# One written order over all blocks, scalings first in their chunk, and a re-dealt second block in a time-mix and FFN kernel

## The chip, the core and the metric

The kernel runs on one NeuronCore of one Trainium2 chip. The metric is the device time of one execution in microseconds (us); lower is better. PE is TensorE (its matmuls; PEld its weight loads), DVE is VectorE, ACT is ScalarE, POOL is GpSimd, and SP (SyncE) issues nearly all of the DMAs. Each engine has its own queue of instructions; between engines semaphores make an instruction wait.

## The reference

The input x has the shape 4 x 1024 x 512 (batch, time, channels); there are 704 hidden channels in the time mix and 2048 in the FFN. Cut to what matters:

```python
xn  = layernorm(x)
xx  = concat([xn[:, 1:2], xn[:, :-1]], axis=1) - xn        # the token before
k   = (xn + xx * time_mix_k) @ Wk.T
r   = (xn + xx * time_mix_r) @ Wr.T
w   = exp(-exp(time_decay))
s_t = s_{t-1} * w + relu(k_t)                              # a scan over time, per hidden channel
o   = layernorm((s * r) @ Wv.T) * ln_gamma + ln_beta
d   = gelu(fp16(xn) @ W0.T + bias0).astype(fp16)
e   = (d @ W1.T + bias1).astype(fp16)
out = x + o + e
```

## The kernel before

The 4096 tokens are worked on in eight blocks of 512 tokens, two to a batch (TB = 512), counted from 0; block i is mixed, projected, scanned and gated, and goes through the FFN. The loop over the blocks has 16 chunks n (NN = 16), one for each 128 of the FFN's hidden channels. In a chunk PE does `up` for the FFN chunk two ahead (AHEAD = 2, 8 matmuls into a bank pd, L784), `down` for chunk n (8 matmuls into the four sums pe, L806) and one piece of the time mix. After the last chunk DVE rounds the four sums pe to fp16 (`rounded`, L763, called e in the profile), which frees them for the next block's first `down`.

A piece is, in blocks from the second on, one of ten `three_pass` projections (bank pa, L626, and bank pb by `product`, L383): k in chunks 0 to 4, r in chunks 7 to 11, with two half passes in chunks 5 and 6. In chunks 12 to 15 the pieces are the four output products: `out_three_pass` (oa, L721; ob, L729 and L731) from the third block on, and `out_full` with `out_halves` in the first two. What follows a piece on ACT and DVE, its `after`, is issued in the chunk behind it: ACT copies pa (L638, or oa at L735), DVE adds pb (L639, or L736), and then come the relu (L641) and the scan (L519) for k, and the gating (L536) for r. The pool `ps_mm` has four PSUM banks for pd, pa, pb, oa and ob; the pool `ps_e` has four more for pe.

Exact fp32 products are made of parts. `split_x` makes three (h by ACT at L284, l and m by DVE at L286 and L288, with a first step at L235), `split_kr` does it for the weights of k and r and stores the parts to DRAM, `split_wv` for those of the output. Parts are tiles of 128 x 512 in buffers of tag "q" (QS of them; a block's states g, raw weights and the FFN's w0h and w0l take them too), and a new part waits until the buffer it gets has been read for the last time. Short-lived fp32 tiles (`temp`) have the tag "s".

The next block, j = i + 1, is made ready in the meantime: x is loaded, DVE takes its statistics, normalizes it, and transposes it in 16 steps into xnT (L331). `x16` has ACT copy xnT to fp16 (L344), `ffn_input` copies that to the FFN's input xf (L379). `mixed` is run for each of four groups of channels c: ACT scales the current token twice (L360), DVE adds the scaled token before (L363 and L367; in the first block of a batch a one-column copy, L352, comes first), and `split_x` follows.

The order on PE, DVE, ACT and SP is the written one, by `manual_schedule`; it holds within a region, and the loop opens one region for each block. Where instructions of two regions fall among each other, and POOL's order, are left to the scheduler. Within a chunk the written order is: `up`, the first step of the followers, Gelu and its cast (L794, L799), `down`, the piece, and then the rest of the followers woven with the chunk's list of background jobs `bg[n]`, which `put(n, ...)` fills.

Of the kernel before, what the change touches and what calls it, by code (L numbers as in the profile page):

```python
# [11 lines left out]
F32 = mybir.dt.float32  # L12
F32R = mybir.dt.float32r
I32 = mybir.dt.int32
AF = mybir.ActivationFunctionType
ALU = mybir.AluOpType

P = 128
# [4 lines left out]
def time_mix_and_gelu_ffn(  # L23
# [30 lines left out]
    nc = tc.nc  # L54
# [3 lines left out]
    TB = 512  # L58
    NS = TB // P
    NC = C // P  # L60
    NN = N // P
    Q = 32
    QS = 63
    RAW_OUT = 2
    S = 4096.0
    MASK = -4096
# [6 lines left out]
    LAST = len(blocks) - 1  # L73
# [5 lines left out]
    const = pool("const", 1)  # L79
# [5 lines left out]
        return wide.tile([P, TB], dtype, tag=tag, name=name, bufs=bufs)  # L85

    def temp(name):
        return const.tile([P, TB], F32, tag="s", name=name, bufs=5)

    def small(shape, tag, name, bufs=2):  # L90
        return const.tile(shape, F32, tag=tag, name=name, bufs=bufs)
# [246 lines left out]
    def half_tile(name):  # L338
        return const.tile([P, TB], F16, tag="h16", name=name, bufs=NS)

    def x16(i):
        for c in range(NC):
            x16s[i, c] = half_tile(f"x16_{i}_{c}")
            nc.scalar.copy(x16s[i, c], xnT[:, c, 1:])  # L344

    def mixed(i, c, meanwhile=lambda: None):
        t0 = blocks[i][1]
        now = xnT[:, c, 1:]
        if t0 > 0:
            nc.gpsimd.tensor_copy(xnT[:, c, 0:1], last[:, c, :])  # L350
        else:
            nc.vector.tensor_copy(xnT[:, c, 0:1], now[:, 0:2][:, 1:2])  # L352
        if t0 + TB < T:
            nc.gpsimd.tensor_copy(last[:, c, :], xnT[:, c, TB : TB + 1])
        prior = xnT[:, c, :TB]
        srcs = []
        for kind in range(2):
            j = kind * NC + c
            srcs.append(temp(f"x{'kr'[kind]}_{i}_{c}"))
            nc.scalar.activation(srcs[kind], now, AF.Identity, scale=rest_sb[:, j : j + 1])  # L360
        xk, xr = srcs
        meanwhile()
        nc.vector.scalar_tensor_tensor(  # L363
            xk, prior, mk_sb[:, c : c + 1], xk, ALU.mult, ALU.add
        )
        yield
        nc.vector.scalar_tensor_tensor(  # L367
            prior, prior, mr_sb[:, c : c + 1], xr, ALU.mult, ALU.add
        )
        xks[i, c] = yield from split_x(xk, f"k_{i}_{c}")  # L370
        xrs[i, c] = prior
# [4 lines left out]
    def ffn_input(i):  # L376
        xf = [part(f"xf_{i}_{c}", tag="xf", bufs=4) for c in range(NC)]
        for c in range(NC):
            nc.scalar.copy(xf[c], x16s.pop((i, c)))  # L379
        return xf  # L380
# [464 lines left out]
    def several(fn, *calls):  # L845
        for args in calls:
            fn(*args)
# [16 lines left out]

    followers = []
    e16s = []
    for i in range(len(blocks)):
        with tc.manual_schedule(
            engines=engines
        ):  # L870
            j = i + 1
            tail = 4 if i == LAST else 0
            by_columns = range(NS // 2, NS) if tail else ()
            pieces, bg = {}, defaultdict(list)

            def put(n, fn, *args):
                bg[n].append(lambda: fn(*args))
# [15 lines left out]

            def turn(first, end):
                transposed(state["x"], first, end)

            def fresh_mixed(c, n):
                if i > 0 and n == NN - AHEAD - 1:
                    return mixed(j, c, next_xf)
                return mixed(j, c)  # L900

            def next_xf():
                state["xf"] = ffn_input(j)

            for s in range(NS):
                pieces[12 + (s // 2 if i == LAST else s), s] = [out_piece, i, s]
            if i == 0:
                state["x"] = x_next
                pieces[1, 0] = [raw_k, i, 3]
                pieces[3, 0] = [raw_r, i, 3]  # L910
                pieces[5, 0] = [raw_k, i, 4]
                pieces[7, 0] = [raw_r, i, 4]
                pieces[9, 0] = [
                    lambda i: raw_halves(i, [bank(f"pkr_{i}_{q}") for q in range(2)]), i
                ]
                put(0, several, split_w0, (1, 2), (1, 3))
                for c in range(NC):
                    put(2 + c - (c == 0), split_w0, 2, c)
                    put(3 + c, load_w0, 3, c)
                    put(5 + c, split_w0, 3, c)  # L920
                put(1, stats, *range(NS))
                put(3, lambda: norm_apply(j, state["x"]))
                for h in range(NF):
                    put(1 + 2 * h, split_kr, 0, h)
                put(4, turn, 0, 1)
                put(5, turn, 1, 5)
                put(7, turn, 5, 10)
                put(8, turn, 10, 11)
                put(9, turn, 11, 16)
                put(4, load_late_constants)  # L930
                put(12, split_half)
                mix_at = (11, 12, 13, 15)
            else:
                order = [(0, h) for h in range(NF)] + [(1, h) for h in range(NF)]
                for k, (kind, h) in enumerate(order):
                    pieces[k + 2 * kind, 0] = [three_pass, i, kind, h]
                    if k > 1:
                        early = (4, 6, 8, 9, 10)[h] if i == kind == 1 else k - 2 + 2 * (k > 6)
                        put(early, fetch_kr, i, kind, h)
                pieces[5, 0] = [half_pass, i, 0]  # L940
                pieces[6, 0] = [half_pass, i, 1]
                for c, n in enumerate((2, 3, 5, 5) if i == 1 else (2, 2, 3, 3)):
                    put(n, split_xr, i, c)
                if j <= LAST:
                    put(2, fetch_x)
                    for s in range(NS):
                        put(4, stats, s)
                    put(6 if i == 1 else 5, lambda: norm_apply(j, state["x"]))
                    turns = (0, 5, 5, 5, 1) if i == 1 else (3, 4, 4, 3, 2)
                    for k in range(sum(turns)):  # L950
                        unit = next(n for n in range(5) if k < sum(turns[: n + 1]))
                        put(6 + unit, turn, k, k + 1)
                mix_at = (12, 13, 15, 15) if i == 1 else (12, 13, 14, 15)
            if i == 1:
                for g in range(NN // G):
                    put(2 * g, store_w0l, g)
                for h, n in enumerate((1, 10, 11, 12, 13, 13)):
                    put(n, split_wv, h)
            put(11 if j <= LAST else 2, fetch_residual)
            if j <= LAST:  # L960
                put(10, x16, j)
                for c, n in enumerate(mix_at):
                    put(n, fresh_mixed, c, n)
                put(13, fetch_kr, j, 0, 0)
                put(14, fetch_kr, j, 0, 1)

            pe = [ps_e.tile([P, C], F32, tag="pe", name=f"pe_{i}_{s}") for s in range(NS)]
            for n in range(NN):
                ahead = n + AHEAD
                if ahead == NN and j <= LAST:  # L970
                    if i == 0:
                        next_xf()
                    xf = state["xf"]
                nxt = (i, ahead) if ahead < NN else (j, ahead - NN)
                gelu = up(*nxt) if nxt[0] <= LAST else None
                works = [follow() for follow in followers]
                if i == 0 or n == NN - NS or (n > NN - NS and i < RAW_OUT):
                    finished(*works)
                    works = []
                else:  # L980
                    works = [w for w in works if next(w, works) is None]
                followers = []
                if gelu:
                    d = gelu()
                if n < NN - tail:
                    operands = waiting.pop(0)
                    for s in range(NS):
                        down(n, s, *operands, end=NN - tail if s in by_columns else NN)
                if gelu and i > 0:
                    waiting.append((d, load_w1(*nxt)))  # L990
                two_on = (i, ahead + 2) if ahead + 2 < NN else (j, ahead + 2 - NN)
                if two_on[0] <= LAST:
                    load_w0l(*two_on)
                jobs = [
                    lambda s=s: finish(i - 1, s, e16s[s])
                    for s in (2 * n, 2 * n + 1)
                    if s < len(e16s)
                ]
                for s in range(NS):
                    if (n, s) in pieces:  # L1000
                        fn, *args = pieces[n, s]
                        followers.append(fn(*args))
                if i == 0 and ahead + 1 < NN:
                    load_w1_raw(ahead + 1)
                woven(works, jobs + bg[n])
                if i == 0:
                    waiting.append((d, load_w1(*nxt)))
                store_weights()
# [60 lines left out]
```

## Time and profile before

| | us |
|---|---|
| median of 3 runs | 886.42 (885.8 to 887.17) |
| the profiled execution | 889.37 |
| its span, first to last instruction | 887.2 |
| the first `down` of blocks 2 to 7 (counted from 0) begins at | 252.29, 357.58, 462.93, 568.25, 673.62, 778.96 |

The last row is from the chain of waits: from block 2 on a block takes 105.3 to 105.4 us. Busy time by stage, where each row is a stretch of the span, followed by the busy time of each engine and the number of its instructions, the granted TensorE clock, the share of the DMA engines and what they moved:

```profile
44.00:137.00 93.00, 92.32 (x361) 59.69 (x360) 68.21 (x113) 50.84 (x87) 4.73 (x10) 1.00 0.68 232
137.00:249.20 112.20, 109.28 (x442) 80.76 (x440) 85.40 (x140) 58.28 (x97) 5.53 (x14) 0.98 0.67 220
453.30:558.60 105.30, 104.96 (x461) 86.01 (x461) 84.36 (x135) 51.41 (x86) 11.72 (x20) 1.00 0.66 225
```

They are most of the first block, the second block, and one of the later ones. The columns of busy time are PE, PEld, DVE, ACT and POOL. A matmul's shown duration (0.39 us) is longer than the distance between the starts of two (0.23 us), so waits of PE are best read from starts.

### The profile page before, as it was taken

To read this page: it belongs to the slowest core of one execution; us is meant where nothing else is said; L and a number is where in the kernel's file an instruction comes from. 1 tells how busy PE (TensorE), PEld (TensorE's weight loads), DVE (VectorE), ACT (ScalarE), POOL (GpSimd) and SP (SyncE) were. 2 spreads that over 40 slices of the span, in tenths; PEclk is the share of its full clock that TensorE was granted. 3 is DMA by queue.
4 is the path that set the end of the run, shared out by engine and by line. 5 is a ranking of instruction groups with operands and counts; after the bars stand their busy time and mean duration, and the time that the engine had idled before them with its cause. 6 is when DMAs were issued, how large, how long until landed. Compare 5 with 4: busy or idle time off the path is not lost.

```text
span 887.2 us, 11092 instructions
## 1 busy us (share of the span) xinstructions
PE 868.7 (98%) x3760; PEld 686.6 (77%) x3760; DVE 671.3 (76%) x1098; ACT 431.5 (49%) x733; POOL 75.2 (8%) x142
## 2 busy tenths in 40 slices
PE   8999999999999999999999999999999999999996
PEld 7676657876668888788878888788887888878885
DVE  4767768697698868878697787877788886884547
ACT  3856653456534455444554445444464445544430
POOL 1100000000012001000112000100011200100001
PEclk8999999999999999999999999999999999999998
DMA  9579755965449675677458775596665966568731
GB/s 261 202 226 326 250 170 177 327 231 192 152 139 353 208 225 175 228 267 243 163 170 300 234 238 190 169 337 197 216 201 182 328 208 223 179 221 279 236 120 48
DMA packets 100164, 195.01 MB, mean 220 GB/s; under 512 B 10991, under 2 KB 25356, under 8 KB 100108
## 3 DMA queue, kind: packets, MB, share of 16 engines
q1 hardware_dynamic: 100048, 194.29, 65.7%
q8 instruction: 30, 0.49, 0.2%
q14 instruction: 26, 0.21, 0.1%
q10 hardware_dynamic: 60, 0.02, 0.0%
HBM read 165.43 MB, written 28.84 MB: 219 GB/s over the span
## 4 chain that ended last, share of the span: by engine, by line
PE 80%; DVE 10%; ACT 4%; DMA 2%; issue 2%; SPq 0%; ACTq 0%; DVEq 0%
PE pd L784 22%; PE pe L806 21%; PE pa L626 13%; PE pb L383 7%; PE oa L721 5%; PE po L682 3%; PE ph L655 2%; PE ob L729 2%; PE pk L383 2%; DVE xnT L331 2%; PE pr L383 1%; PE ob L731 1%; ACT d L794 1%; DMA wvraw<-in_L_attn_Wv 1%; DVE e L763 1%
## 5 line engine op out<-in xcount | busy, mean ns | idle before, releaser
L806 PE MATMUL pe<-w,d 128*128 128x512 f32 x1008 | 252.5, 392 | 3.3 <-DVE e L763 1.7
L806 PEld LDWEIGHTS pe<-w,d 128*128 128x128 f32 x1008 | 187.2, 188 | 49.5 <-DVE e L763 9.2
L784 PE MATMUL pd<-xf,w0h 128*128 128x512 f32 x512 | 204.5, 399 | 0.3 <-ACT xf L379 0.3
L784 PE MATMUL pd<-xf,w0l 128*128 128x512 f32 x512 | 199.9, 390 | 0.0
L794 ACT ACTIVATE d<-pd,late_sb 128x512 f16<-128x512 f32 x128 | 87.7, 685 | 131.7 <-PE pd L784 131.4
L784 PEld LDWEIGHTS pd<-xf,w0h 128*128 128x128 f32 x512 | 96.5, 189 | 27.1 <-issue 4.1
L784 PEld LDWEIGHTS pd<-xf,w0l 128*128 128x128 f32 x512 | 96.6, 189 | 21.7 <-issue 1.9
L639 DVE SCALAR_TENSOR_TENSOR y<-pb,a 128x512 f32<-128x512 f32 x70 | 48.3, 690 | 66.7 <-PE pb L383 52.3
L638 ACT ACTIVATE a<-pa 128x512 f32<-128x512 f32 x70 | 41.7, 596 | 86.6 <-PE pa L626 86.6
L799 ACT CAST d<-d 128x512 fp32r<-128x512 f16 x128 | 79.5, 621 | 4.1
L331 DVE STREAM_TRANSPOSE xnT<-x 32x512 f32<-32x512 f32 x112 | 78.6, 702 | 2.0
L299 POOL TENSOR_SCALAR ry<-mvy 128x1 f32<-128x1 f32 x32 | 20.2, 630 | 436.2 <-DVE mvy L306 436.2
L626 PE MATMUL pa<-hk,kr 128*128 128x512 f32 x140 | 54.5, 390 | 0.0
L626 PE MATMUL pa<-lk,kr 128*128 128x512 f32 x140 | 54.5, 389 | 0.0
L363 DVE SCALAR_TENSOR_TENSOR xk<-xnT,mix_sb,xk 128x512 f32<-128x512 f32 x28 | 21.1, 752 | 34.1 <-ACT xk L360 34.0
L626 PE MATMUL pa<-hr,kr 128*128 128x512 f32 x120 | 46.7, 389 | 0.0
L721 PE MATMUL oa<-wv,lg 128*128 128x512 f32 x120 | 46.7, 389 | 0.0
L721 PE MATMUL oa<-wv,hg 128*128 128x512 f32 x120 | 46.7, 389 | 0.0
L626 PE MATMUL pa<-lr,kr 128*128 128x512 f32 x120 | 46.7, 389 | 0.0
L641 ACT ACTIVATE y<-y 128x512 f32<-128x512 f32 x35 | 22.1, 633 | 49.4 <-DVE y L639 49.4
L519 DVE TENSOR_TENSOR_SCAN g<-late_sb,carry,y 128x512 f32<-128x512 f32 x20 | 25.7, 1284 | 18.3 <-ACT y L641 13.3
L383 PE MATMUL pb<-mk,kr 128*128 128x512 f32 x140 | 37.4, 389 | 0.0
(166 smaller groups left out, 1348.7 us busy)
## 6 DMA issues: line engine op xcount, KB each, us to landing
w<-w1d SPq DMA_DIRECT2D x110, 512.0 KB, 3.7
kr<-krd SPq DMA_DIRECT2D x195, 256.0 KB, 4.9
w0l<-w0d SPq DMA_DIRECT2D x96, 256.0 KB, 4.0
x<-in_L_attn_x SPq DMA_DIRECT2D x32, 256.0 KB, 6.0
w1d<-w SPq DMA_DIRECT2D x16, 512.0 KB, 2.9
xres<-in_L_attn_x SPq DMA_DIRECT2D x32, 256.0 KB, 5.3
krd<-wt SPq DMA_DIRECT2D x30, 256.0 KB, 3.2
out<-xres SPq DMA_DIRECT2D x28, 256.0 KB, 4.6
```

Source lines behind the costliest of these rows:

```text
L331: nc.vector.transpose(dst[i * Q : (i + 1) * Q, :, :, j, :], src[j * Q : (j + 1) * Q, :, :, i, :],)
L383: return nc.tensor.matmul(dst, w[:, c, :], src, start=(c == 0), stop=(c == NC - 1))
L519: nc.vector.tensor_tensor_scan(dst[:hw], w_sb[:hw, h : h + 1].to_broadcast([hw, TB]), src[:hw], 0.0 if t0 == 0 else carry[:hw, h : h + 1], ...
L626: nc.tensor.matmul(pa, w[p][:, c, :], xs[j, c][p], start=(c == 0 and p == 0), stop=(c == NC - 1 and p == 1),)
L638: nc.scalar.activation(a, pa, AF.Copy, scale=1.0 + 1.0 / S)
L639: nc.vector.scalar_tensor_tensor(y, pb, -1.0 / S, a, ALU.mult, ALU.add)
L682: nc.tensor.matmul(pos[s], gs[i, h][:, s * P : (s + 1) * P], wv_raw[h], start=(h == 0), stop=False,)
L721: nc.tensor.matmul(pa, gs[i, h][p][:, cols], wv[h][p], start=(h == 0 and p == 0), stop=(h == NF - 1 and p == 1),)
L784: nc.tensor.matmul(pd, w, xf[c], start=(c == 0 and p == 0), stop=(c == NC - 1 and p == 1),)
L794: nc.scalar.activation(d16, pd, AF.Gelu, bias=b0_sb[:, n : n + 1])
L799: nc.scalar.copy(d, d16)
L806: nc.tensor.matmul(pe[s] if sum_ is None else sum_, d[:, s * P : (s + 1) * P], w1[p][:, cols], start=(n == first and p == 0), stop=(n == e ...
```

## The change

All blocks now stand in one `manual_schedule` region, so that the written order holds from block to block. `mixed` loses its two scalings; they become `scaled_now`, which is issued at the head of the chunk, ahead of the followers and Gelu, except where two groups are mixed in one chunk: there the second is scaled just before it is mixed. The fp16 copies are put two to a chunk (chunks 10 and 11 in the first block, 11 and 12 later; all four in chunk 10 before). `ffn_input` is run in chunk 13 behind Gelu (in chunk 14 ahead of `up` in the first block before, and inside `mixed` in chunk 13 in the others). In the second block (i == 1) the splits of r's input go to chunks 1, 2, 3, 4 (2, 3, 5, 5 before), its statistics to chunks 4 and 5 two each (all to 4 before), the first split of Wr to 5 (4 before) and the first of Wv to 7 (1 before). One buffer moves from tag "q" (63 to 62) to tag "s" (5 to 6).

```diff
-    QS = 63
+    QS = 62
...
     def temp(name):
-        return const.tile([P, TB], F32, tag="s", name=name, bufs=5)
+        return const.tile([P, TB], F32, tag="s", name=name, bufs=6)
...
-    def x16(i):
-        for c in range(NC):
-            x16s[i, c] = half_tile(f"x16_{i}_{c}")
-            nc.scalar.copy(x16s[i, c], xnT[:, c, 1:])
-
-    def mixed(i, c, meanwhile=lambda: None):
+    def x16(i, c):
+        x16s[i, c] = half_tile(f"x16_{i}_{c}")
+        nc.scalar.copy(x16s[i, c], xnT[:, c, 1:])
+
+    parts_now = {}
+
+    def scaled_now(i, c):
+        parts_now[i, c] = [temp(f"x{k}_{i}_{c}") for k in "kr"]
+        for kind, dst in enumerate(parts_now[i, c]):
+            j = kind * NC + c
+            nc.scalar.activation(
+                dst, xnT[:, c, 1:], AF.Identity, scale=rest_sb[:, j : j + 1]
+            )
+
+    def mixed(i, c):
...
-        srcs = []
-        for kind in range(2):
-            j = kind * NC + c
-            srcs.append(temp(f"x{'kr'[kind]}_{i}_{c}"))
-            nc.scalar.activation(srcs[kind], now, AF.Identity, scale=rest_sb[:, j : j + 1])
-        xk, xr = srcs
-        meanwhile()
+        xk, xr = parts_now.pop((i, c))
...
-    for i in range(len(blocks)):
-        with tc.manual_schedule(
-            engines=engines
-        ):
+    with tc.manual_schedule(engines=engines):
+        for i in range(len(blocks)):
...
-            pieces, bg = {}, defaultdict(list)
+            pieces, bg, early = {}, defaultdict(list), defaultdict(list)
...
-            def fresh_mixed(c, n):
-                if i > 0 and n == NN - AHEAD - 1:
-                    return mixed(j, c, next_xf)
-                return mixed(j, c)
-
-            def next_xf():
-                state["xf"] = ffn_input(j)
...
-                        early = (4, 6, 8, 9, 10)[h] if i == kind == 1 else k - 2 + 2 * (k > 6)
-                        put(early, fetch_kr, i, kind, h)
+                        first = (5, 6, 8, 9, 10)[h] if i == kind == 1 else k - 2 + 2 * (k > 6)
+                        put(first, fetch_kr, i, kind, h)
...
-                for c, n in enumerate((2, 3, 5, 5) if i == 1 else (2, 2, 3, 3)):
+                for c, n in enumerate((1, 2, 3, 4) if i == 1 else (2, 2, 3, 3)):
                     put(n, split_xr, i, c)
...
-                        put(4, stats, s)
+                        put(4 + s // 2 if i == 1 else 4, stats, s)
...
-                for h, n in enumerate((1, 10, 11, 12, 13, 13)):
+                for h, n in enumerate((7, 10, 11, 12, 13, 13)):
                     put(n, split_wv, h)
...
-                put(10, x16, j)
+                for c in range(NC):
+                    put((10 if i == 0 else 11) + c // 2, x16, j, c)
                 for c, n in enumerate(mix_at):
-                    put(n, fresh_mixed, c, n)
+                    if n == mix_at[c - 1]:
+                        put(n, scaled_now, j, c)
+                    else:
+                        early[n].append((j, c))
+                    put(n, mixed, j, c)
...
                 if ahead == NN and j <= LAST:
-                    if i == 0:
-                        next_xf()
-                    xf = state["xf"]
+                    xf = next_xf
                 nxt = (i, ahead) if ahead < NN else (j, ahead - NN)
                 gelu = up(*nxt) if nxt[0] <= LAST else None
+                several(scaled_now, *early[n])
                 works = [follow() for follow in followers]
...
                 if gelu:
                     d = gelu()
+                if ahead + 1 == NN and j <= LAST:
+                    next_xf = ffn_input(j)
```

`mix_at` (the chunks of the four mixings) is unchanged: 11, 12, 13, 15 in the first block, 12, 13, 15, 15 in the second and 12, 13, 14, 15 later.

## The prediction

> **What bounds the kernel now.** I read the page first (engine shares, chain), then the chain in order of time, then the time lines of PE, VectorE (DVE) and ScalarE (ACT) around every place where PE's matmuls leave their normal pitch.
>
> ```profile
> PE 868.7 (98%) x3760; PEld 686.6 (77%) x3760; DVE 671.3 (76%) x1098; ACT 431.5 (49%) x733; POOL 75.2 (8%) x142
> PE 80%; DVE 10%; ACT 4%; DMA 2%; issue 2%; SPq 0%; ACTq 0%; DVEq 0%
> ```
>
> PE is the bound; eight matmuls of 512 columns take 1.81 us in the chain, 0.227 us each. So only the places where PE waits can be won. Adding up each start-to-start distance above its form's median, I find: block 0 near 87 us 0.7 (a w1 split, untouched) and near 117 us 0.5; block 1 near 177 us 1.0, near 193 us 0.4, near 210 us 3.9; the boundary from block 1 to 2 1.6; the five boundaries 2-3 to 6-7 0.93 each. Some 13 us, 1.5%, is all there is. The largest, PE first, then ACT:
>
> ```profile
> 209.93 0.39 PE L626 MATMUL pa<-lr,wt 128*128 128x512 f32 x1
> 212.38 1.80 PE L383 MATMUL pb<-mr,wt 128*128 128x512 f32 x4 [2.06 <-ACT a L638]
> ```
> ```profile
> 208.41 0.62 ACT L266 CAST wv<-vu 128x512 fp32r<-128x512 f32 x1 [1.29 <-DVE vu L235]
> 209.14 0.63 ACT L267 ACTIVATE wv<-vd 128x512 fp32r<-128x512 f32 x1
> 209.68 2.16 ACT L344 CAST x<-xnT 128x512 f16<-128x512 f32 x4
> 211.75 0.58 ACT L638 ACTIVATE a<-pa 128x512 f32<-128x512 f32 x1
> ```
>
> pb needs one of four PSUM buffers, freed by the `a` copy (L638) of the piece before. That copy stands behind four fp16 copies (L344) and a wv split, and the split waits for a late DVE. Why DVE is late is seen 45 us earlier:
>
> ```profile
> 160.87 0.69 DVE L639 SCALAR_TENSOR_TENSOR y<-pb,a 128x512 f32<-128x512 f32 x1 [1.90 <-PE pb L383]
> 166.53 1.28 DVE L519 TENSOR_TENSOR_SCAN g<-late_sb,carry,y 128x512 f32<-128x512 f32 x1 [4.97 <-PE pb L383]
> ```
>
> The scan has its input at 161.9 but nowhere to write: the 63 buffers of tag "q" are full, and the next one is freed by PE's pb of chunk 4. My count for block 1: w0h 16, w0l 16, raw wv 6, raw Wr 5, xk 12, so 8 are free (the last block's states are done); state 0, wv 0 (3), state 1, xr 0 (3), state 2 and xr 1 (3) take those 8 and the 4 w0l given back, and state 3, the 13th, waits. DVE then runs almost without a gap until 210 us.
>
> The later boundaries, DVE then PE:
>
> ```profile
> 562.53 0.75 DVE L363 SCALAR_TENSOR_TENSOR xk<-xnT,mix_sb,xk 128x512 f32<-128x512 f32 x1 [0.56 <-ACT xk L360]
> ...
> 565.70 0.69 DVE L286 TENSOR_TENSOR lk<-xk,uk 128x512 fp32r<-128x512 f32 x1
> 566.31 0.68 DVE L736 SCALAR_TENSOR_TENSOR oy<-ob,oa 128x512 f32<-128x512 f32 x1
> 566.91 0.68 DVE L288 SCALAR_TENSOR_TENSOR mk<-lk,uk 128x512 fp32r<-128x512 f32 x1
> 567.51 2.47 DVE L763 TENSOR_TENSOR e<-pe,b_sb 128x512 f16<-128x512 f32 x4
> ```
> ```profile
> 568.25 2.54 PE L806 MATMUL pe<-w,d 128*128 128x512 f32 x8 [0.34 <-DVE e L763]
> ```
>
> PE needs the first rounding e at 567.75; it ends at 568.20. Before it stand the 0.56 us wait for the scaling and L736, which belongs to the next block: the scheduler slipped it in between two separately ordered regions.
>
> **What the Trainium skill says.** "PSUM — Partial Sum Buffer", section "Engine vs sequencer instructions": the queues of ScalarE, VectorE and GpSimd are strict FIFO. The trace agrees: `a` at 211.75 waits behind copies it doesn't need. "TensorE: Matmul & The Clock Gate", section "What's actually happening": the clock is halved after an idle window of about 3.4 us, and the window is free-running. Here 2.2 us of idling was enough: after 212.38 the pitch is 0.427 us for eight matmuls (1.7 us lost), while 0.9 us at 177 and 1.2 us at 251 cost nothing of the kind. "ScalarE: Activation LUTs", section "Table sets: the hidden batching unit": identity, copy and relu stand in every table set, so an Identity moved ahead of a Gelu costs no table load; Gelu and L360 follow each other here at gaps of 0.00 to 0.03 us.
>
> **The change, part by part.**
>
> *fp16 copies two to a chunk, xf made in chunk 13.* No instruction is added. In block 0 xf is ready before chunk 14: PE's 0.34 us wait at 117.76 and the slow steps behind it (0.17) go: -0.5. In block 1 the four L344 leave chunk 10: ACT reaches `a` 2.07 us sooner, all else equal. In later blocks `a` in chunk 10 loses a 2 us delay that PE never felt: 0.
>
> *One written order.* At each boundary e comes before L736: DVE reaches e 0.60 us sooner, L736 comes later, but its PSUM bank isn't needed for over 2 us. POOL stays the scheduler's; SP's order at the boundaries hardly changes: 0.
>
> *Scaling first.* Two L360 (0.62 us apart) now stand ahead of `oa`, in ACT's queue behind hk of the chunk before. In chunk 15 of block 1 DVE now idles 4.07 us for L360 behind a Gelu; scaled early, mixing 2 starts some 4 us sooner, and mixing 3, whose scaling stays late, about 3. The roundings then end before PE's 251: -1.6.
>
> In blocks 2 to 6 it trades waits. DVE gains 0.56 in chunks 14 and 15 and 1.1 in 12 and 13, but oy now waits for oa: from uk's start, hk after 0.45, L360 after 0.53, the second after 0.62, oa after 0.62, its end and release 0.63: 2.85 us, against 1.79 us for DVE to be free itself. One turn is oy to uk 5.05 (0.71+0.73+0.22+0.67 to L363, 0.67+0.78+0.61+0.66 on to uk), plus 0.18 where POOL's rstd (1.53 us after the aggregate) is now last: 5.23+2.85 = 8.08 us, in a chunk of 7.48. So DVE enters chunk 13 some 0.9 us ahead but oy stays at 544.06 (before 544.04), then 552.13 (552.08), 560.19 (559.56). From there without waits: uk 565.42, e at 567.21, against 567.51. PE gains 0.3 us at the three boundaries into odd blocks. Into even blocks L352 (0.25 us to L363) is no longer covered in four chunks; with POOL's wait absorbed e falls at 567.7: loss 0.17, twice. Together -0.6. The sixth temp buffer covers the early L360: with five temporaries to a chunk it writes buffers read out a chunk before. Both ends: -4.7 (all five stalls gone, oa not in the way) and +5.5 (e 1.1 us late each time).
>
> *Block 1 dealt out anew.* xr 0 to 3 go to chunks 1 to 4, wv 0 to 7, split of Wr 0 to 5. The q count with 62 buffers: 7 free + 4 returned = 11; state 0, xr 0 (3), state 1, xr 1 (3), state 2, two parts of xr 2 take them. The third, mr of xr 2 in chunk 3, waits for the same pb of chunk 4. So DVE stands from about 159 to 166.5 with y of piece 3 behind it, and behind y the relu and Gelu on ACT. y then ends at 167.85; the up of chunk 5, due at 166.94, needs its bank: +1.0. DVE goes on: mr, y, scan with relu (2.7), xr 3 (1.9), two stats (1.6), y and scan (2.7), Wr 0 (1.85), two stats (1.6), y, scan, Wr 1, normalizing: y of the second half pass at 185.3, where it is at 185.13 now. The hr wait at 177 goes (-1.0), the one at 193 too (-0.4). But chunk 7 now has five transposes (3.6) and then wv 0 (1.85), whose two ACT halves end at 192.3; `a` of piece 0 of r stands behind them, ending 192.8 instead of 185.8, and PE's pb wants that bank at 190.6: +2.3. From there DVE is busy to chunk 10: Wr 4 and wv 1 give `a` at 212.8 where it was 212.33, without the four copies but with wv 0 and the later start. PE stands 0.9 to 1.0 there, or, if the stall at 191 halves the clock (+1.7[...]), not at all. On SP, the three stores of Wr 0 now wait in chunk 5 until 177.6, and behind them the w1 that down needs at 187; the rstd of the spread stats (POOL, 1.5 us) is ready some 3 us before normalizing: 0 for both. In later blocks 33 parts of w0h and wv and at most 28 others are in use, so the buffer given up costs nothing there. Before 5.3; after 1.1+2.35+1.0 = 4.4, or 1.1+2.35+1.7 = 5.15: -0.2 to -0.9; I take -0.5. Ends: -5.3 (no stall left), +2.
>
> Sum: -0.5 -0.5 -1.6 -0.6 = -3.2 us. Against the profiled execution (889.37 with a span of 887.2) that is 886.2; the runs' median, 886.42, lies 2.95 lower, so 883.2.
>
> **Rivals.** *A: the new deal empties block 1.* If mr finds a buffer in chunk 3, DVE is on time in chunk 7, wv 0 is done by 188 and all 5.3 us go: 886.42-0.5-5.3-1.6-0.6 = 878.4. For it: nothing but this wait makes DVE late. Against: the count that explains 166.53 exactly. *B: nothing.* DVE bounds block 1 as before and the clock drops: block 1 +1, later boundaries +1: 886.42-0.5+1-1.6+1 = 886.3. *C, slower: the ring hk, two L360, oa, oy.* At five boundaries each microsecond that e is later costs one. Speaking for it: the turn of 8.08 against 7.48; against it: the lead from chunk 12. It outweighs the other 2.6 us from 0.52 us late; at 1.1 us it gives 886.42-2.6+5.5 = 889.3. *D: the order isn't kept* (the scheduler still slips L736 in): +0.6 a boundary, 886.2, counted with B.
>
> **Numbers.** Forecast 42%, own range 881.5 to 885.0; A 18%, B with D 17%, C 23%. 877.5 to 889.0 leaves out about half of C and a little of A. This kernel's runs tell 0.2% (1.8 us) from no change: faster 0.60, within 0.17, slower 0.23.
>
> **What would show it.** DVE's wait of some 7 us before L288 near 159 us; PE waits near 167 and 191 us and less than 1 us near 212; `a` ending near 192.8; no PE wait at 117 and 251; L763 straight after L288 at each boundary; DVE waiting about 1 us at L736 on oa in chunks 14 and 15. Wrong if PE still stalls 2 us near 210, if nothing waits at 159 and 191 (A), or if PE's wait at the later boundaries exceeds 0.5 us (C).

## The result, and the profile after

The changed kernel takes 890.98 us (median of 4 runs, 890.31 to 893.21) against 886.56 (885.8 to 887.17) for the kernel before in the same series: ratio 1.0055, 95% interval 1.0035 to 1.0075. It is slower; 883.2 had been forecast, with 889.0 as the upper end. The profiled execution took 890.49 us with a span of 888.7.

The page's engine line and the engine shares of its chain of waits, after:

```profile
PE 867.3 (98%) x3760; PEld 687.3 (77%) x3760; DVE 674.6 (76%) x1098; ACT 429.2 (48%) x733; POOL 81.4 (9%) x142
PE 80%; DVE 11%; ACT 4%; POOL 2%; issue 2%; DVEq 0%; ACTq 0%
```

Nothing was added, and the shares hardly move. Two things do: POOL is busy 6.2 us longer (75.2 before) with the same 142 instructions, and it now appears in the chain with 2%. That is the first hint.

Next, where the time went. Each block is measured from its first `down` (the first matmul into pe) to the next block's (block 7 to its last matmul into pe), both kernels from the profile:

| us | before | after | difference |
|---|---|---|---|
| block 0 | 96.66 | 95.59 | -1.07 |
| block 1 | 115.26 | 113.52 | -1.74 |
| block 2 | 105.29 | 105.45 | +0.16 |
| blocks 3, 4, 5, 6 | 105.35, 105.32, 105.37, 105.34 | 106.77, 106.03, 106.77, 106.02 | +1.42, +0.71, +1.40, +0.68 |
| block 7 | 95.53 | 95.54 | 0 |

Blocks 2 to 6 together take 526.67 us before and 531.04 after: +4.37. Everything gained in the first two blocks (2.8 us) is lost there, and some 1.5 us more. The stretches of the table of busy times (length, then busy time and number of instructions of PE, PEld, DVE, ACT, POOL, then clock, DMA share, GB/s) for blocks 1, 3 and 4 of the kernel after:

```profile
135.86:249.38 113.52, 110.81 (x450) 82.40 (x448) 89.68 (x147) 58.90 (x98) 4.97 (x13) 0.98 0.65 218
354.83:461.60 106.77, 105.00 (x460) 86.05 (x461) 85.68 (x138) 51.02 (x86) 9.67 (x14) 1.00 0.65 222
461.60:567.63 106.03, 105.01 (x461) 86.06 (x461) 84.72 (x134) 50.98 (x86) 12.81 (x20) 1.00 0.65 223
```

Clock 1.00, DVE at 80% and DMA at 65%: no engine but PE is full in blocks 3 and 4, and PE's busy time is 1 to 1.8 us below the length. So something waits in a chain. PE's waits, in its time line after (start, duration, instruction, and in brackets the idle time ahead of it and what ended it):

```profile
166.65 0.50 PE L786 MATMUL pd<-xf,w0h 128*128 128x512 f32 x1 [0.71 <-DVE y L641]
...
191.61 1.71 PE L385 MATMUL pb<-mr,wt 128*128 128x512 f32 x4 [2.00 <-ACT a L640]
193.12 0.63 PE L786 MATMUL pd<-xf,w0h 128*128 128x512 f32 x1
...
567.63 0.73 PE L808 MATMUL pe<-w,d 128*128 128x512 f32 x2 [1.02 <-DVE e L765]
...
674.40 1.09 PE L808 MATMUL pe<-w,d 128*128 128x512 f32 x3 [1.78 <-DVE e L765]
```

The first two stand where the prediction put them. The 0.63 at 193.12 instead of 0.39 is the halved clock (granted 0.50 from 192.1 to 195.5, 1.7 us lost). The last two are the loss: by the distance of starts, PE's first `down` is late by 1.18 us into blocks 3, 5 and 7 and by 1.93 to 1.95 into blocks 4 and 6. Before, it was 0.50 at each. All of these wait for e.

Why e is late is read on DVE, one turn from oy to oy (the time line after, chunks 14 and 15 of block 4):

```profile
551.05 0.69 DVE L738 SCALAR_TENSOR_TENSOR oy<-ob,oa 128x512 f32<-128x512 f32 x1 [0.95 <-ACT oa L737]
551.77 0.69 DVE L305 BATCH_NORM_STATS2 sty<-oy 128x6 f32<-128x512 f32 x1
552.50 0.18 DVE L306 BATCH_NORM_AGGREGATE mvy<-sty 128x2 f32<-128x6 f32 x1
552.72 0.75 DVE L710 SCALAR_TENSOR_TENSOR oy<-oy,mvy,gamma_sb 128x512 f32<-128x512 f32 x1
553.39 0.75 DVE L365 SCALAR_TENSOR_TENSOR xk<-xnT,mix_sb,xk 128x512 f32<-128x512 f32 x1
554.60 0.75 DVE L715 SCALAR_TENSOR_TENSOR oy<-oy,ry,beta_sb 128x512 f32<-128x512 f32 x1 [0.46 <-POOL ry L300]
...
556.66 0.42 DVE L235 TENSOR_SCALAR uk<-xk 128x512 int32<-128x512 int32 x1
...
559.49 0.69 DVE L738 SCALAR_TENSOR_TENSOR oy<-ob,oa 128x512 f32<-128x512 f32 x1 [0.95 <-ACT oa L737]
...
566.28 0.69 DVE L288 SCALAR_TENSOR_TENSOR mk<-lk,uk 128x512 fp32r<-128x512 f32 x1
566.89 1.28 DVE L765 TENSOR_TENSOR e<-pe,b_sb 128x512 f16<-128x512 f32 x2
```

and ACT's part of the same turn:

```profile
557.11 0.62 ACT L284 CAST hk<-uk 128x512 fp32r<-128x512 f32 x1 [4.03 <-DVE uk L235]
557.64 0.72 ACT L351 ACTIVATE xk<-xnT,rest_sb 128x512 f32<-128x512 f32 x1
558.27 0.71 ACT L351 ACTIVATE xr<-xnT,rest_sb 128x512 f32<-128x512 f32 x1
558.88 0.57 ACT L737 ACTIVATE oa<-oa 128x512 f32<-128x512 f32 x1
```

It is the ring of rival C: uk, hk, two scalings, oa, oy, and back through POOL's ry to uk. Each step waits for the one before it or stands behind it in its engine's queue, and the uk at the end starts the next turn. A turn takes 559.49 - 551.05 = 8.44 us while a chunk of PE takes 7.48. ACT's side, uk to oy, is 559.49 - 556.66 = 2.83 us (2.85 was predicted). The other side, oy to uk, is 5.61 against a predicted 5.23. What differs there is the 0.46 us ahead of L715. POOL, before and then after (L300 is the pow of the output's layernorm):

```profile
561.27 0.78 POOL L299 TENSOR_SCALAR ry<-mvy 128x1 f32<-128x1 f32 x1 [6.05 <-DVE mvy L306]
562.14 0.57 POOL L300 TENSOR_TENSOR ry<-ry,nhalf 128x1 f32<-128x1 f32 x1
```
```profile
552.77 0.78 POOL L299 TENSOR_SCALAR ry<-mvy 128x1 f32<-128x1 f32 x1 [6.64 <-DVE mvy L306]
553.64 0.93 POOL L300 TENSOR_TENSOR ry<-ry,nhalf 128x1 f32<-128x1 f32 x1
...
660.04 1.11 POOL L300 TENSOR_TENSOR ry<-ry,nhalf 128x1 f32<-128x1 f32 x1
```

The add ahead of it (L299) takes 0.78 us in both kernels here. The pow on 128 numbers takes 0.57 us before and 0.93 or 1.11 after. Before, it starts at 562.14 in the 0.56 us in which DVE waits for the scaling (L363 starts at 562.53). That gap is what the change filled. Now L365 has begun when the pow starts, and the pow ends 0.43 us after L365 does: at 554.57 with L365 ending at 554.14. Ahead of blocks that begin a batch, the one-column copy comes before L365, more of L365 is left, and the pow grows by as much, to 1.11 us. The Trainium skill, "SBUF — State Buffer", section "Who interferes with whom", says that a DVE instruction with two SBUF inputs contends with a GpSimd instruction that reads SBUF, and calls the ports that the two share an exclusive lock. L365 reads xnT and xk, both in SBUF, so this fits.

The same trace holds a comparison that tells this from DVE being busy at all. In the first two blocks L710 reads po, a PSUM bank; from the third block on the same line reads oy, a tile in SBUF, in the same shape and time:

```profile
231.71 0.75 DVE L710 SCALAR_TENSOR_TENSOR o<-po,mvy,gamma_sb 128x512 f32<-128x512 f32 x1
231.76 0.22 POOL L299 TENSOR_SCALAR ry<-mvy 128x1 f32<-128x1 f32 x1 [21.21 <-DVE mvy L306]
232.07 0.57 POOL L300 TENSOR_TENSOR ry<-ry,nhalf 128x1 f32<-128x1 f32 x1
...
877.88 0.74 DVE L710 SCALAR_TENSOR_TENSOR oy<-oy,mvy,gamma_sb 128x512 f32<-128x512 f32 x1
878.13 0.92 POOL L300 TENSOR_TENSOR ry<-ry,nhalf 128x1 f32<-128x1 f32 x1
```

Beside L710 with its PSUM input the add takes 0.22 us, and the pow 0.57, all eight times, though L710 has 0.39 us or more left when the pow starts. Beside L710 with both inputs in SBUF the pow takes 0.92, and the add 0.78 (at 552.77, beside L710 at 552.72). So it matters where DVE's inputs lie, and the add had been paying the same price in the kernel before.

### The profile page after: what moved, and what is told of

It is laid out like the page before. It is cut to its first block, busy times and chain, and to the rows that moved or that the text cites. A ratio compares the mean times of both kernels' runs of the same rounds, so it can differ in the third digit from the quotient of the medians.

```text
span 888.7 us, 11076 instructions
## 1 busy us (share of the span) xinstructions
PE 867.3 (98%) x3760; PEld 687.3 (77%) x3760; DVE 674.6 (76%) x1098; ACT 429.2 (48%) x733; POOL 81.4 (9%) x142
## 4 chain that ended last, share of the span: by engine, by line
PE 80%; DVE 11%; ACT 4%; POOL 2%; issue 2%; DVEq 0%; ACTq 0%
PE pd L786 22%; PE pe L808 22%; PE pa L628 13%; PE pb L385 7%; PE po L684 4%; PE oa L723 3%; PE ph L657 2%; PE pk L385 2%; PE pr L385 2%; PE ob L731 1%; POOL ry L300 1%; DVE oy L715 1%; DVE xnT L369 1%; DVE sty L305 1%; POOL ry L299 1%
## 5 line engine op out<-in xcount | busy, mean ns | idle before, releaser
L640 ACT ACTIVATE a<-pa 128x512 f32<-128x512 f32 x70 | 41.8, 597 | 86.4 <-PE pa L628 86.4
L299 POOL TENSOR_SCALAR ry<-mvy 128x1 f32<-128x1 f32 x32 | 19.8, 619 | 431.2 <-DVE mvy L306 431.2
L284 ACT CAST hk<-uk 128x512 fp32r<-128x512 f32 x28 | 17.4, 621 | 56.9 <-DVE uk L235 56.9
```

What stands on the lines that cost most here:

```text
L299: nc.gpsimd.tensor_scalar_add(r, var, EPS)
L640: nc.scalar.activation(a, pa, AF.Copy, scale=1.0 + 1.0 / S)
```

## The experiments

Each was run 4 to 16 times, in a series with the kernel before, whose medians were 887.43 (experiments 1 to 4), 886.79 (5 to 8) and 887.21 (9 and 10). The ratios are estimated from the runs of a series and need not equal the quotient of two medians. The last two columns are lengths in the profiled run, from a block's first `down` to the next one's:

| | time | ratio to before (95%) | block 1 | blocks 2 to 6 |
|---|---|---|---|---|
| before | | | 115.26 | 526.67 |
| after | 890.98 | 1.0055 (1.0035 to 1.0075) | 113.52 | 531.04 |
| 1 scaling as its own late job | 898.54 | 1.0109 (1.0089 to 1.0129) | 113.61 | 538.97 |
| 2 scaling behind oa | 879.51 | 0.9904 (0.9884 to 0.9924) | 112.86 | 521.33 |
| 3 eps added on DVE | 882.76 | 0.9938 (0.9922 to 0.9953) | 113.50 | 523.92 |
| 4 before, one order only | 885.44 | 0.9972 (0.9961 to 0.9983) | 114.82 | 524.83 |
| 5 scaling in `mixed`, xf not | 894.89 | 1.0082 (1.0067 to 1.0097) | 113.63 | 534.00 |
| 6 = 2, wv 0 in chunk 14 | 876.96 | 0.9884 (0.9869 to 0.9900) | 110.56 | 521.33 |
| 7 = 6, xr 2 in chunk 4 | 874.57 | 0.9857 (0.9842 to 0.9872) | 108.77 | 521.33 |
| 8 = 2, 63 buffers | 877.44 | 0.9887 (0.9872 to 0.9903) | 110.94 | 521.33 |
| 9 scaling and xf back | 887.27 | 1.0001 (0.9993 to 1.0010) | 115.41 | 526.83 |
| 10 = 7 with 3 | 875.59 | 0.9865 (0.9847 to 0.9882) | 108.74 | 521.33 |

521.33 is five times 104.27, but for rounding: the length of a block in which PE never waits. In the profiled runs of before, after, 3 and 4 block 1 holds one stretch of halved clock, some 1.7 us; in the others it holds none.

**1. The scaling put back late, as a job of its own.**

```diff
-                    if n == mix_at[c - 1]:
-                        put(n, scaled_now, j, c)
-                    else:
-                        early[n].append((j, c))
+                    put(n, scaled_now, j, c)
                     put(n, mixed, j, c)
```

> The changed kernel with the scaling L360/L351 back where it was, in mixing, behind Gelu and its cast; all else as changed. Ring theory (two scalings between hk and oa make oy late, and the pow on POOL, now beside L365, makes L715 late): the waits of PE at the five later boundaries fall from 1.63 and 2.38 us to about 0.3 each, the pow takes 0.57 us again, the boundary of blocks 1 and 2 takes back about 0.8: 890.98 - 8 + 1 = 884 us (882.5 to 885.5). Rival, one region: the order over the boundaries makes DVE late in the next chunk and costs by itself: stays at 889 or more. Rival, block 1's new deal is the loss: stays at 889 or more.

A miss: 898.54, slower still. A job of its own is woven one step later, so L365 falls behind L715, which waits 0.77 us for POOL (its pow takes 0.57 us here), and in chunk 13 the scaling stands behind the four copies of xf (DVE waits 2.20 us for it). This did not undo the change, it made a third order; it tells only how much hangs on the order inside a chunk: 19 us lie between this and the next. Some 5 us of them, in the profiled run, are three stretches of halved clock behind its waits (granted 0.52 to 0.55 near 465, 574 and 684).

**2. The scaling behind oa.** It is still in the chunk ahead of Gelu, but behind the followers' first step, so that it leaves the ring.

```diff
-                several(scaled_now, *early[n])
                 works = [follow() for follow in followers]
...
                 followers = []
+                several(scaled_now, *early[n])
                 if gelu:
                     d = gelu()
```

> The changed kernel with the scaling still early in its chunk, but behind the first step of what follows a piece (so ACT's order is hk, oa, two scalings, Gelu). Ring theory: oa is ready 1.6 us after uk's start, before DVE is free (1.79), the turn is 6.84 + 0.46 for POOL = 7.3 us, under the chunk's 7.48, so the waits at the five boundaries nearly vanish: 890.98 - 9 = 882 us (881 to 884). If POOL's pow and not the ring is what makes e late: the pow stays long and PE still waits about 1 us at each: 887 or more.

879.51 us, more than the expected 882: all waits at the later boundaries are gone. ACT and then DVE in its time line:

```profile
550.75 0.62 ACT L284 CAST hk<-uk 128x512 fp32r<-128x512 f32 x1 [2.93 <-DVE uk L235]
551.27 0.59 ACT L737 ACTIVATE oa<-oa 128x512 f32<-128x512 f32 x1
551.76 0.71 ACT L351 ACTIVATE xk<-xnT,rest_sb 128x512 f32<-128x512 f32 x1
```
```profile
551.47 0.69 DVE L288 SCALAR_TENSOR_TENSOR mk<-lk,uk 128x512 fp32r<-128x512 f32 x1
552.16 0.69 DVE L738 SCALAR_TENSOR_TENSOR oy<-ob,oa 128x512 f32<-128x512 f32 x1
...
555.72 0.75 DVE L715 SCALAR_TENSOR_TENSOR oy<-oy,ry,beta_sb 128x512 f32<-128x512 f32 x1 [0.46 <-POOL ry L300]
```

oy follows L288 at once, and L715 still waits 0.46 us for POOL (whose pow takes 0.92 us here too). So the longer pow costs nothing where the ring doesn't go through oa: it takes both.

**3. The other side of the ring shortened.** In the changed kernel DVE adds eps, so POOL only has the pow to do.

```diff
-        rstd = rstd_of(mv[:, :, 1], f"ry_{i}_{s}")
+        rstd = small([P, 1], "rstd1", f"ry_{i}_{s}")
+        nc.vector.tensor_scalar_add(rstd, mv[:, :, 1], EPS)
+        nc.gpsimd.tensor_tensor(rstd, rstd, nhalf[:, :1], ALU.pow)
```

> The changed kernel with the addition of eps in the output's layer norm moved from POOL to DVE (one 128x1 instruction more on DVE per output tile, one fewer on POOL), so the pow ends before L365. If POOL's wait (0.46 us at L715 in each chunk into odd blocks, more into even ones) is part of the turn: the turn falls from 8.44 to about 8.1, e is about 1 us earlier at each boundary, 890.98 - 5 = 886 us (885 to 888). If the ring hk, scalings, oa alone is the cause and POOL's wait only takes up slack: same within 1 us.

882.76 us, 8.2 below the changed kernel by the medians and 7.1 by the stretch of blocks 2 to 6. DVE's time line:

```profile
547.23 0.69 DVE L740 SCALAR_TENSOR_TENSOR oy<-ob,oa 128x512 f32<-128x512 f32 x1 [0.95 <-ACT oa L739]
...
548.90 0.15 DVE L708 TENSOR_SCALAR ry<-mvy 128x1 f32<-128x1 f32 x1
...
550.29 0.74 DVE L717 SCALAR_TENSOR_TENSOR oy<-oy,ry,beta_sb 128x512 f32<-128x512 f32 x1
...
555.16 0.69 DVE L740 SCALAR_TENSOR_TENSOR oy<-ob,oa 128x512 f32<-128x512 f32 x1 [0.95 <-ACT oa L739]
```

The ring is there as before (0.95 us of waiting for oa), but ry is ready when L717 (L715 above) comes, and a turn is 555.16 - 547.23 = 7.93 us instead of 8.44. Half a microsecond less, three times in a row, takes away 7.1 of the 9.7 us by which blocks 2 to 6 of the changed kernel exceed five blocks without a wait. What is left into blocks 4 and 6 is 0.46 us of waiting, into 3, 5 and 7 none over 0.15. More was won than expected (886).

**4. The kernel before with one region alone.**

```diff
-    for i in range(len(blocks)):
-        with tc.manual_schedule(
-            engines=engines
-        ):
+    with tc.manual_schedule(engines=engines):
+        for i in range(len(blocks)):
```

> The kernel before with nothing but one region over all blocks. If the written order is a gain by itself (e 0.6 us earlier at each boundary, no L736 between lk and mk): the waits at the five boundaries fall from 0.93 to about 0.3 and the one of blocks 1 and 2 from 1.6 to about 0.9: 886.56 - 4 = 882.5 us (881.5 to 884.5). Rival, one region costs: 886.5 or more.

885.44: the one order gains 1.84 us in blocks 2 to 6, some 0.37 at each boundary (the wait ahead of PE's first `down` falls from 0.50 to 0.03), and is no part of the loss. The total fell short of the expectation by 2.9 us: in block 1 nothing is gained but 0.44, and block 2 has a new wait of 0.32 us at 280.9.

**5. The two scalings called inside `mixed`, all else as changed.**

```diff
+        scaled_now(i, c)
         xk, xr = parts_now.pop((i, c))
...
-                    if n == mix_at[c - 1]:
-                        put(n, scaled_now, j, c)
-                    else:
-                        early[n].append((j, c))
```

> The changed kernel with the two scalings put back inside mixing, directly ahead of L365, where they stood before (so L365 again comes ahead of L715 on DVE, unlike in the run with the scaling as a job of its own). Ring theory with POOL: DVE idles ahead of L365 again, the pow runs in that gap in 0.57 us, L715 waits for nothing, e comes 0.6 us earlier than in the kernel before because the order over the boundary is kept: waits at the five boundaries 0.44 each, the one of blocks 1 and 2 back at about 1.2: 890.98 - 7.5 + 1.2 = 884.7 us (883 to 886). If the early scaling isn't the loss: 889 or more.

A miss: 894.89. In the kernel before the scaling of chunk 13 stood ahead of the copies of xf; the change moved xf up behind Gelu, and with the scaling back in `mixed` the copies come first. ACT and DVE in its time line:

```profile
545.10 2.18 ACT L382 CAST xf<-x 128x512 fp32r<-128x512 f16 x4
547.19 0.72 ACT L351 ACTIVATE xk<-xnT,rest_sb 128x512 f32<-128x512 f32 x1
```
```profile
547.94 0.75 DVE L366 SCALAR_TENSOR_TENSOR xk<-xnT,mix_sb,xk 128x512 f32<-128x512 f32 x1 [2.10 <-ACT xk L351]
```

Behind two of its waits the clock is halved besides (granted 0.50 near 570 and 785), some 3 us in the profiled run. So the early xf needs the early scaling: the parts of the change are coupled, and undoing one alone is not the kernel before.

**9. Scaling and xf both put back** (one order, copies two to a chunk and the new deal stay):

```diff
-    def mixed(i, c):
+    def mixed(i, c, meanwhile=lambda: None):
...
+        scaled_now(i, c)
         xk, xr = parts_now.pop((i, c))
+        meanwhile()
...
-                    if n == mix_at[c - 1]:
-                        put(n, scaled_now, j, c)
-                    else:
-                        early[n].append((j, c))
-                    put(n, mixed, j, c)
+                    put(n, fresh_mixed, c, n)
...
-                if ahead + 1 == NN and j <= LAST:
-                    next_xf = ffn_input(j)
+                if i == 0 and ahead + 1 == NN:
+                    make_xf()
```

Here `fresh_mixed` passes `make_xf`, which calls `ffn_input`, to the mixing of chunk 13 from the second block on.

> The changed kernel with the scaling put back whole: the two scalings are called inside `mixed`, ahead of its first DVE step, and ffn_input again behind the scaling of chunk 13 (from the second block on); all else stays changed (one order over the blocks, two fp16 copies to a chunk, block 1 dealt out anew, 62 + 6 buffers). If scaling first is what made the later boundaries slow (the ring over POOL and oa), those boundaries come back to the 0.4 to 0.5 us that the kernel before with one order alone has (0.44 each); the boundary 1 to 2 keeps some 0.8 to 1.2 us; about 884.5 us, so 6 below the changed kernel. If the slow boundaries come from another part of the change (one order, the copies, the buffers), the time stays near 891. In chunks 14 and 15 of the later blocks the pow on POOL takes 0.57 us again where DVE idles for the scaling.

887.27: 3.7 below the changed kernel, so scaling first with xf is the loss, but 2.8 above the expectation. Blocks 2 to 6 fall from 531.04 to 526.83, with PE's wait 0.58 into odd blocks and under 0.15 into even ones. Block 1 loses what the early scaling had gained: it now has 1.6 us more at 228.5 (waiting for xf) and 0.76 at the boundary to block 2, and block 2 0.34 at 281.5. POOL's part of the expectation was half wrong: into even blocks the pow takes 0.57 us, but into odd blocks L367 here (L365 above) starts right before the pow, which takes 1.01 to 1.04 us, and L717 waits 0.46 for it. Those are the boundaries with the 0.58, so the longer pow may well cost something here; no run took it out of this version.

**8, 6 and 7: block 1, on top of experiment 2.** One buffer back (63, and 5 temporaries); the first split of Wv in chunk 14; and with that the third split of r's input in chunk 4:

```diff
-    QS = 62
+    QS = 63
...
-        return const.tile([P, TB], F32, tag="s", name=name, bufs=6)
+        return const.tile([P, TB], F32, tag="s", name=name, bufs=5)
```
```diff
-                for h, n in enumerate((7, 10, 11, 12, 13, 13)):
+                for h, n in enumerate((14, 10, 11, 12, 13, 13)):
...
-                for c, n in enumerate((1, 2, 3, 4) if i == 1 else (2, 2, 3, 3)):
+                for c, n in enumerate((1, 2, 4, 4) if i == 1 else (2, 2, 3, 3)):
```

> The version with the scalings behind oa, with the buffer given back: 63 of tag q, 5 of tag s; block 1 dealt out as in the change. The count says: 12 buffers are free to be had in chunks 1 to 3, xr 2 takes the last, and state 3 (the 13th) waits in chunk 4 as in the kernel before. So the wait at 165 us (0.87) goes, DVE is 1.4 us earlier in chunk 7, the one at 189 falls from 2.15 to about 0.8: 879.5 - 2.2 = 877.3 us (876 to 879). If the five temporaries are too few for the early scaling: no gain or a loss, with PE waiting at the later boundaries.

> The version with the scalings behind oa, and block 1's first split of Wv in chunk 14 instead of 7. If wv 0 is what holds the copy L640 back in chunk 7: PE's wait near 189 us (2.15) and the one near 210 (0.82) vanish, the wait of 0.87 at 165 stays: 879.5 - 3 = 876.5 us (875.5 to 878). If DVE's backlog alone decides: the wait moves to chunk 11 with 1 to 2 us: 878 to 879.5.

> As the run with wv 0 in chunk 14, and r's third split (xr 2) in chunk 4 instead of 3, so that the part that must wait for a buffer of tag q stands behind y and the scan of piece 3 and not ahead of them. If the buffers explain PE's wait near 165 us: it vanishes too, DVE still waits about 3.5 us for a buffer in chunk 4: 875.5 us (874.5 to 877). If that wait has another cause: as the run without it.

With one buffer more, mr of xr 2 starts at 156.62 with no wait and PE's wait of 0.87 us at 165 is gone, 2.15 at 189 becomes 1.24: the count of buffers holds. Five temporaries were enough there: no wait shows at the later boundaries. With wv 0 moved away, the waits at 189 and 210 are gone, but a new one of 0.71 us ends at 193.03, for a w1 load that SP issued at 186.57, behind stores, and that landed at 192.99; in the versions with the stall at 189 PE came to it later. In experiment 7 this wait is gone as well, so not all that 7 gains over 6 is the buffer. With both moves nothing over 0.15 us above the usual is left on PE from 137 us on, except the steps at block 1's output products that every version has (0.41 to 0.46 each), and the time is 874.57: the fastest, 1.4% below the kernel before. All three came within 1 us of what was expected.

**10. Experiment 7 with eps on DVE** (the diff of experiment 3).

> The kernel with the scalings behind the followers' first step, the first split of Wv in chunk 14 and the third split of r's input in chunk 4 (874.57 us), with DVE in place of POOL adding eps in the output layernorm. There no PE wait at the later boundaries is left, so POOL's path should bound nothing and the time should be the same, 874.6 within 0.7 us. If POOL's lengthened pow still cost something there, about 1 us would be won.

875.59 (874.88 to 876.12): its runs lie wholly above those of experiment 7, by 1.0 us of the medians where 0.7 had been allowed. But its stretch of blocks 2 to 6 is the same 521.33, and in the profiled runs the difference lies ahead of block 1 (1.7 us later there). At the later boundaries nothing is won, because nothing waits there any more.

## Why the prediction was wrong

**Right, part by part.** *Block 0*: the wait at 117 is gone (-0.5 as said); the rest of its 1.07 us is the wait near 87 for w1, which comes and goes from one profiled run to the next and was not forecast. *One written order*: e follows L288 at once (566.28, 566.89). *Boundary 1 to 2*: no wait is left there. *Block 1*: DVE stands from 157.08 to 165.30 ahead of L288 (foreseen: 159 to 166.5), PE waits 0.87 (1.0) near 167 and 2.16 (2.3) near 191, and near 212 not at all since the clock halved. The lines of DVE and, for the second wait, of ACT, with `a` (L640) behind the halves of wv 0:

```profile
165.30 0.69 DVE L288 SCALAR_TENSOR_TENSOR mr<-lr,ur 128x512 fp32r<-128x512 f32 x1 [8.22 <-PE pb L385]
```
```profile
189.72 0.62 ACT L266 CAST wv<-vu 128x512 fp32r<-128x512 f32 x1 [5.44 <-DVE vu L235]
190.44 0.63 ACT L267 ACTIVATE wv<-vd 128x512 fp32r<-128x512 f32 x1
190.98 0.58 ACT L640 ACTIVATE a<-pa 128x512 f32<-128x512 f32 x1
```

Both blocks with the boundary took 2.81 us less; 2.6 had been forecast. Part of that agreement is luck: 0.58 of the 2.81 is the wait near 87. Which branch block 1 took was luck too: where the clock wasn't halved (experiments 1, 2, 5 and 9, the same 2.15 us at 189) PE did wait 0.80 to 0.83 at 210, the other branch of that sentence. One reading of the trace before was loose, and nothing hung on it: between Gelu and L360 the cast L799 stands each time.

**The step that failed** is in "Scaling first": "oy to uk 5.05 ... plus 0.18 where POOL's rstd (1.53 us after the aggregate) is now last: 5.23+2.85 = 8.08 us". The ring was the right mechanism, with ACT's side right to 0.02 us; the term for POOL was mis-sized. Ry was ready 1.89 us after the aggregate and not 1.53, the term measured 5.61 - 5.05 = 0.56, and a turn is 8.44. Three times this side of the ring lies between the mixing of chunk 12 and the boundary: 3 x 0.36 = 1.1 us, and PE's wait into odd blocks is 1.18 us where 0.2 had been left. For even blocks the prediction let POOL's wait absorb L352 (0.25); the one-column copy (0.18 in the turn) made the pow 0.19 longer instead, and L715 went on waiting 0.46; 1.93 stands where 0.67 had been put. In sum blocks 2 to 6 changed by +4.37 us for a forecast of -0.6.

The mistake was to carry a duration over from the trace before (rstd 1.53 us after the aggregate) into a place where its neighbour is another one: it had been measured in exactly the DVE gap that the change was to fill. Rival C had named the ring and its place and stood at 23%; its price (5.5) was near.

**A second term**: "the runs' median, 886.42, lies 2.95 lower, so 883.2". Against its own profiled execution the sum gave 886.2 and 890.49 was measured, 4.3 more; the other 3.5 us of the miss are this conversion and the 0.5 by which the median lies above that execution. The profiled run of the kernel before was one with a halved clock in block 1; of 51 runs of it beside the experiments, the 13 with a mean clock of 0.992 or less have a median of 889.08 and the other 38 of 886.8. The changed kernel has such a stall of its own (2.16 us at 189), and three of its four runs show 0.992 or less. So most of the 2.95 us was probably a cost that its typical run keeps, and should not have been taken off.

**Shown and argued.** Shown: the loss lies in blocks 2 to 6; breaking the ring (2) or shortening its other side (3) takes it away and more; in experiment 2 the longer pow costs nothing, and with experiment 7 as the base taking time off POOL's path wins nothing (10). In 9 it may cost something. That POOL's add and pow are held back by DVE instructions with two SBUF inputs is the skill's reading; the two forms of L710 show that it is the place of the inputs that counts, within one kernel. No run moved the inputs of L365 itself. What made the time ahead of block 1 differ between profiled runs was not followed up.

## What to carry to other kernels

When a move fills an idle gap, ask which other engine did its work in that gap, and don't use the durations it had there: the short POOL pow here took 0.57 us beside a DVE instruction that read PSUM and up to 1.11 beside one that read two SBUF tiles. A copy put ahead of another in one queue is free only until the results of both close a ring; compare one full turn, with every engine on it, with the period of the bound engine, and put the early work behind the copy that the ring needs. Before a sum is moved from a profiled run to a median, see whether what sets that run apart is a cost that the changed kernel still has.

## What the hardware showed that was not expected

A POOL pow on 128 x 1 numbers took 0.57 us with DVE idle at its start, and also beside L710 with its input in PSUM and 0.39 to 0.46 us left. It took 0.87, 0.93, 1.02 or 1.11 us when a DVE instruction with two SBUF inputs had 0.44, 0.50, 0.6 or 0.69 us left: each time it ended 0.43 us after DVE's end (in experiment 3, beside L712, 0.39 us after). L365 kept its 0.75 us either way.

The clock did not answer to the length of a stall alone. In the profiled runs the same wait at 189 us, 2.15 to 2.16 us long, halved it in the changed kernel and in experiment 3 (from 192 to 195 us) and left it alone in experiments 1, 2, 5 and 9. At the later boundaries a wait of 1.79 us (ending at 571.51 in experiment 1) and two of 1.94 (567.98 and 782.21 in 5) were followed by a halved clock, another of 1.94 (354.97 in 5) and two of 1.93 to 1.95 in the changed kernel were not. This would fit the free-running window that the Trainium skill states ("TensorE: Matmul & The Clock Gate", "What's actually happening"), but each of these stalls is shorter than the 3.4 us given there.
